# A fused attention and expert kernel on one core: first weights in quarters from SyncE, two sequences' pieces moved up, and a pair's scatters side by side

## The chip, the cores and the metric

The kernel runs on one core of a Trainium2 chip. The metric is the device time of one execution in microseconds. Three runs of the kernel before are the base: 709.80, 710.92 and 712.75 us, median 710.92. One more execution was taken with the hardware profiler; its trace gives every duration below.

The engines are called PE (TensorE), DVE (VectorE), ACT (ScalarE), POOL (GpSimd) and SP (SyncE, which issues most of the DMAs). Each runs its own instructions in order and waits on semaphores for the others.

## What is computed

Four sequences of 512 tokens with 256 features go through a conditional gated layer, attention with 16 heads that share one key and value head, a mixed linear layer, and a routed layer of eight experts. Cut to what matters:

```python
expert = argmax(cond_8)                       # one expert per sequence
hidden = silu(x @ Wu[expert].T + bu) * (x @ Wg[expert].T + bg)
c = hidden @ Wd[expert].T + bd                # 256 -> 512 -> 256
q, k, v = c @ Wq.T + bq, ...                  # 16 query heads, one k, one v
x = x + softmax(q k^T / 4) v @ Wo.T + bo
y = x @ mix(weight * mask, cond_8) + bias     # a weight matrix per sequence
probs = softmax(y @ w_router)                 # 8 experts, 2 per token
# in each of 8 groups of 256 tokens an expert takes at most 128 (token, choice) rows
out = x + sum over the kept choices of prob * (gelu(y @ wi[e]) @ wo[e])
```

The host lays out weights (transposes, halves side by side) before the launch; the arithmetic is on the chip.

## The kernel before, in words

All matrices are 32-bit floats. One mm() shows in the trace as two matmul passes and two weight loads.

**Start (lines 88 to 270).** SP loads the eight conditions of each sequence into cond_sb. DVE works out rows, the row numbers of each sequence's expert in the weight table (lines 109 to 117). fetch_cond(b) (line 137) lets POOL gather that expert's up and gate weights (1 MB, tile w, from the pool wi_sb) and its down weights with biases (0.5 MB, tile w2, shown as wo_sb) by an indirect DMA. For b = 0, 1 and 2 these come first on POOL, ahead of POOL's memsets and tables; b = 3 comes later, once tiles of b = 0 are free (wexp has three buffers). SP loads the four sequences of xT, the mask and the eight matrices w2_sb of the mixed layer, the small constants, and last writes zeros over the DRAM table xp (8,580 KB).

hidden(b, hc) makes a quarter of the hidden layer of a sequence: four mm into bank "a" (a single PSUM bank, line 262) and bank "x" (four banks, line 264), a SiLU on ACT (line 266), and a product on DVE (line 267). down(b, dc) (line 248) is the second matrix. Between them DVE mixes weights: mixed(b, g) (lines 235 and 237) adds one of eight masked matrices, which POOL has multiplied with the mask (line 227), into wb_sb. project(b) makes q, k and v of a sequence; SP copies the q rows into their place (line 314).

**Attention (64 steps).** A step n is a quarter of a unit u = n // 4 (four heads of a sequence). Each step runs maxima (PE line 354, DVE line 358) six steps ahead, exponentials (PE line 386, ACT line 387), and weigh of the step before (PE line 401, into bank "a"). At a unit's end its sums are copied to a tile called stage (line 409) and stored to od. shifted(u) (lines 368 and 372) turns the maxima of a unit and adds them to q; exponentials of that unit need its result qs.

Beside the steps run pieces of the neighbouring sequences. The list beside says which piece goes to which of a sequence's 16 steps, last the same for the last sequence (steps 48 to 63), where the pieces (-1, ...) are those of sequence 2. A sequence's chain is values, inv, norm, out, rT, mix (the mixed layer), choose and rank (the router, lines 529 to 567), places (a count by matmul, line 578), rows, send (POOL scatters the tokens to xp by expert, line 630, eight indirect DMAs). pairs is list_of_pairs: DVE lists the tiles of 256 rows (lines 797 to 850) that are full after three sequences, and SP reads the table into a register (lines 877 and 889) to fetch weights (line 870) and rows xt (line 892).

**Experts.** run() goes over units: six pairs (256 rows) of the first three sequences, then 14 single tiles (128 rows), then five more pairs. A unit is turn (PE line 925, DVE line 927), up (PE line 940, ACT line 944), and put for each half (PE line 970): DVE weighs the result (line 978), and POOL adds it to out_rows in DRAM by an indirect DMA (line 979). adds holds these DMAs: each waits for the one before, since both may touch the same rows. share(u) (lines 959 to 963) works out weights and the rows at. The last sequence's pieces go between the first pairs: place() is called twice in a unit's up and once after each put, and final says which pieces come at which call. Its piece rest makes the lists of the remaining tiles and lets the late fetches go.

Of the kernel before, what the change touches and what calls it, by code (L numbers as in the profile page):

```python
# [10 lines left out]
F32 = mybir.dt.float32  # L11
I32 = mybir.dt.int32
AF = mybir.ActivationFunctionType
# [4 lines left out]
P = 128  # L18
B = 4
T = 512  # L20
NT = B * T
D = 256
NE = 8
# [3 lines left out]
F = 1024  # L27
# [10 lines left out]
WROW = 1024 + 10  # L38
# [3 lines left out]
def adaln_attn_ffn_kernel(  # L42
# [34 lines left out]
    def bank(tag):  # L77
        return ps.tile([P, 512], F32, tag=tag, name=f"ps_{tag}", bufs=BANKS[tag])
# [11 lines left out]
    )  # L90


    rev = const.tile([P, NE], F32, name="rev")
    nc.gpsimd.iota(
        rev, pattern=[[-1, NE]], base=NE, channel_multiplier=0,
# [10 lines left out]
    rows = const.tile([P, B], I32, name="rows")  # L106
# [25 lines left out]
    def fetch_cond(b):  # L132

        w = wexp.tile([P, 2, F], F32, name="wi_sb").rearrange("p c f -> p (c f)")
        w2 = wexp.tile([P, F // P, D], F32, name="wo2_sb").rearrange("p c f -> p (c f)")
        for t, src in ((w, wcond), (w2[:, 0:WROW], wcond2)):
            nc.gpsimd.indirect_dma_start(
                out=t,
                out_offset=None,
                in_=src,  # L140
                in_offset=bass.IndirectOffsetOnAxis(ap=rows[:, b : b + 1], axis=0),
            )
        w_of.append((w, w2))

    for b in range(B):
        nc.sync.dma_start(xT_sb[:, :, ts(b, T)], xT[:, :, ts(b, T)])
        if b < 3:
            fetch_cond(b)
    nc.sync.dma_start(m2_sb, mask2.rearrange("p c o -> p (c o)"))
    for g in range(NE):  # L150
        nc.sync.dma_start(w2_sb[:, g, :], w2[:, g].rearrange("p c o -> p (c o)"))

    def load(ap, shape, name):
        t = const.tile(shape, F32, name=name)
        nc.sync.dma_start(t, ap)
        return t
# [95 lines left out]

    def hidden(b, hc):
        w, w2 = w_of[b]
        wu = w[:, 0:1024].rearrange("p (c h) -> p c h", c=2)
        wg = w[:, 1024:2048].rearrange("p (c h) -> p c h", c=2)
        if hc == 0:
            hid_of[b] = cp.tile([P, 4, T], F32, name="hid")
        pu = bank("a")
        pg = bank("x")  # L260
        for c in range(2):
            mm(pu, wu[:, c, ts(hc, P)], xT_sb[:, c, ts(b, T)], start=c == 0, stop=c == 1)  # L262
        for c in range(2):
            mm(pg, wg[:, c, ts(hc, P)], xT_sb[:, c, ts(b, T)], start=c == 0, stop=c == 1)  # L264
        sg = cp.tile([P, T], F32, name="sg", bufs=3)
        nc.scalar.activation(sg, pu, AF.Silu, bias=w2[:, 1024 + hc : 1025 + hc])
        nc.vector.scalar_tensor_tensor(  # L267
            hid_of[b][:, hc, :], pg, w2[:, 1028 + hc : 1029 + hc], sg, ALU.add, ALU.mult
        )

    for b in range(B - 1):
        for hc in range(4):
            hidden(b, hc)
            if (b, hc) > (1, 0):
                for _ in range(4):
                    mixed(*mixing.pop(0))
            if hc == 0 and b > 0:
                down(b - 1, 0)
                down(b - 1, 1)
# [9 lines left out]
    pa_of = {}  # L289
# [102 lines left out]
    def weigh(n, js):  # L392

        u, sc = divmod(n, 4)
        b, hg = divmod(u, 4)
        if u not in pa_of:
            pa_of[u] = bank("a")
        e = e_of[n]
        j0, nj = js[0], len(js)
        for hh in range(4):  # L400
            i = mm(  # L401
                pa_of[u][32 * hh : 32 * hh + 32, j0 * P : (j0 + nj) * P], seqs[b]["v"][:, sc, :],
                e[:, hh, j0 : j0 + nj].rearrange("p j n -> p (j n)"),
                start=sc == 0 and j0 > 0, stop=sc == 3 and j0 == 0,
            )
# [260 lines left out]
    def route_mixed(b):  # L666
# [58 lines left out]
    ON_PE = ("q", "k", "v", "out", "rT", "mix")  # L725
# [15 lines left out]
    def side(b, k):  # L741
# [38 lines left out]
    fp = attn_ctx.enter_context(tc.tile_pool(name="fp", bufs=2))  # L780
# [6 lines left out]
    pairs = fp.tile([P, 3, NE + 1], F32, name="pairs", bufs=1)  # L787
# [75 lines left out]
    reg, adds = {}, []  # L863
# [87 lines left out]
    def share(u):  # L951

        w = width(u)
        number, e0, p0, p1 = (xt_of[u][:, 0:w, D + k] for k in range(4))
        te = texp[:, u : u + 1]
        w0 = fp.tile([P, 2], F32, name="w0", bufs=3)[:, 0:w]
        w1 = fp.tile([P, 2], F32, name="w1")[:, 0:w]
        at = fp.tile([P, 2], I32, name="at", bufs=6)[:, 0:w]
        nc.vector.scalar_tensor_tensor(w0, e0, te, p0, ALU.is_equal, ALU.mult)
        nc.vector.scalar_tensor_tensor(w1, e0, te, p1, ALU.not_equal, ALU.mult)  # L960
        nc.vector.tensor_tensor(w0, w0, w1, ALU.add)  # L961
        nc.vector.tensor_scalar(w1, number, 0.0, spare1, ALU.is_equal, ALU.mult)  # L962
        nc.vector.scalar_tensor_tensor(at, number, -1.0, w1, ALU.add, ALU.add)  # L963
        shares[u] = w0, at

    def put(u, h):

        po = bank("x")
        for fc in range(F // P):
            mm(  # L970
                po[:, 0:D], hT_of[u][:, fc, ts(h, P)], wo_of[u][:, fc, :],
                start=fc == 0, stop=fc == F // P - 1,
            )
        if h == 0:
            share(u)
        w0, at = shares[u]
        y = fp.tile([P, D], F32, name="y", bufs=6)
        nc.vector.tensor_scalar(y, po[:, 0:D], w0[:, h : h + 1], None, ALU.mult)  # L978
        i = nc.gpsimd.indirect_dma_start(  # L979
            out=out_rows,  # L980
            out_offset=bass.IndirectOffsetOnAxis(ap=at[:, h : h + 1], axis=0),
            in_=y,
            in_offset=None,
            compute_op=ALU.add,
        )

        if adds:
            tc.add_manual_dep(i.ins, adds[-1].ins.name, AFTER, reason="same rows")
        if u < NA:
            tc.declare_no_dep(i.ins, group="last rows", reason="other sequences")  # L990
            tc.add_to_no_dep_group("early adds", i.ins)
        elif u == first_of_rest[0] and h == 0:
            for k in last_rows:
                tc.add_manual_dep(i.ins, k.ins.name, AFTER, reason="rows of the last sequence")
        adds.append(i)

    for n in range(STEPS + 1):
        m = n + LEAD
# [2 lines left out]
        b, k = divmod(n, 16)  # L1001
# [40 lines left out]
    places = itertools.count()  # L1042
# [71 lines left out]
def _layouts(i):  # L1114
# [32 lines left out]
    return {  # L1147
        "xT": halves(i["x"].reshape(NT, D).T),
        "cond": i["cond_8"].reshape(1, B * NE),
        "wcond": np.concatenate([up, gate], axis=1),  # L1150
        "wcond2": np.concatenate([down, b_up, b_gate, b_down], axis=1),
        "wq": halves(i["L0_attn_Wq"].T),
        "bq": i["L0_attn_bq"].reshape(2, P).T,
# [38 lines left out]
```

## Time and profile before

| what | us |
|---|---|
| median of three runs | 710.92 |
| the profiled execution | 722.33 |
| its span, first to last instruction | 720.50 |
| TensorE matmuls busy in the span | 669.3 |
| first matmul | 15.20 |
| first projection (line 307) | 72.48 |
| first unit of the experts (line 925) | 428.02 |
| end of the last matmuls | 703.2 |
| start of the last scatter (line 979) | 707.64 |

The profiled execution is 11.4 us longer than the median; it is set against its own parts. A row of the timeline gives the start and the time in us, the engine, the line, the operation with output<-input, its shape and count, and in brackets the engine's idle time before it with what ended that. In the 40 slices each stands for 18.0 us; a digit is the busy share in tenths, PEclk the granted TensorE clock.

### The profile page before, as it was taken

How to read it: one execution, taken by the hardware profiler on the slowest of the kernel's cores; microseconds unless marked ns; L12 is line 12 of the kernel's file. 1: busy time of each engine (PE TensorE's matmuls, PEld its weight loads, DVE VectorE, ACT ScalarE, POOL GpSimd, SP SyncE). 2: the span in 40 equal slices, each digit the busy share in tenths (PEclk: the TensorE clock that was granted, in tenths of full speed). 3: DMA queues.
4: the chain of work that ended last, by engine and by line, in shares of the span. 5: the costliest groups of instructions: out<-in, count | busy, mean ns of one | idle time of the engine just before them, and what ended most of it. 6: DMA issues, size and time to landing. Idle time of an engine off the chain costs nothing. (4 is left out here: it accounts for less than half of the span.)

```text
span 720.5 us, 10657 instructions
## 1 busy us (share of the span) xinstructions
PE 669.3 (93%) x4092; PEld 409.9 (57%) x4092; DVE 325.8 (45%) x760; ACT 226.8 (31%) x401; POOL 116.0 (16%) x119
## 2 busy tenths in 40 slices
PE   1999999999999999999989869999899999999990
PEld 0444433444344433453325338888799999988880
DVE  0246465566667693767766821536122222211210
ACT  0222113566554454455443642131111111121110
POOL 6600000000000013000400220126221112122221
PEclk9999899999999998999989989999999999999995
DMA  8997101100031104110221289734889999985321
GB/s 301 330 291 219 30 1 31 28 16 26 15 90 53 45 19 129 63 60 16 66 86 60 63 272 313 217 89 118 278 225 307 327 322 336 327 243 150 82 23 16
DMA packets 62184, 102.38 MB, mean 142 GB/s; under 512 B 6320, under 2 KB 26416, under 8 KB 61616
## 3 DMA queue, kind: packets, MB, share of 16 engines
q1 hardware_dynamic: 53840, 85.56, 36.7%
q0 software_dynamic: 7872, 15.29, 9.0%
q10 hardware_dynamic: 416, 0.79, 0.4%
q8 instruction: 34, 0.56, 0.3%
q14 instruction: 22, 0.18, 0.1%
HBM read 75.37 MB, written 24.15 MB: 138 GB/s over the span
## 5 line engine op out<-in xcount | busy, mean ns | idle before, releaser
L358 DVE TENSOR_REDUCE negm<-ps_m 128x1 f32<-128x512 f32 x250 | 160.9, 685 | 91.2 <-PE ps_x L386 69.2
L387 ACT ACTIVATE e<-ps_x 128x512 f32<-128x512 f32 x244 | 132.7, 595 | 130.7 <-PE ps_x L386 115.8
L354 PE MATMUL ps_m<-k,q 32*128 32x512 f32 x500 | 157.5, 651 | 5.4 <-DVE negm L358 3.4
L386 PE MATMUL ps_x<-qs,k 32*128 32x512 f32 x488 | 144.0, 657 | 0.3 <-DVE qs L372 0.3
L940 PE MATMUL ps_m<-xT,wi_sb 128*128 128x128 f32 (+1 forms) x800 | 132.0, 323 | 1.6 <-ACT e L944 0.8
L970 PE MATMUL ps_x<-wo_sb,e 128*128 128x256 f32 x576 | 130.0, 382 | 0.0
L940 PEld LDWEIGHTS ps_m<-xT,wi_sb 128*128 128x128 f32 x800 | 120.1, 193 | 12.2 <-ACT e L944 1.0
L970 PEld LDWEIGHTS ps_x<-wo_sb,e 128*128 128x128 f32 x576 | 108.6, 192 | 14.0
L944 ACT ACTIVATE e<-ps_m 128x512 f32<-128x512 f32 x72 | 42.9, 597 | 209.5 <-PE ps_m L940 203.4
L979 POOL DMA_INDIRECT out_dram<-y,at x36 | 55.8, 1550 | 211.2 <-DMA out_dram<-y,at 97.5
L354 PEld LDWEIGHTS ps_m<-k,q 32*128 32x128 f32 x500 | 45.9, 186 | 64.1 <-issue 29.3
L401 PE MATMUL ps_a<-e,v 128*32 128x256 f32 x1024 | 74.8, 392 | 2.7 <-ACT stage L409 2.3
L927 DVE COPY xT<-ps_a 128x256 f32<-128x256 f32 (+1 forms) x25 | 13.6, 542 | 117.7 <-PE ps_a L925 115.7
L401 PEld LDWEIGHTS ps_a<-e,v 128*32 128x32 f32 x1024 | 24.3, 109 | 73.4 <-issue 56.2
L978 DVE TENSOR_SCALAR y<-ps_x,w 128x256 f32<-128x256 f32 x36 | 17.4, 483 | 82.1 <-PE ps_x L970 80.9
L262 PE MATMUL ps_a<-xT_sb,wi_sb 128*128 128x512 f32 x64 | 34.1, 659 | 15.2 <-DMA wi_sb<-in_wcond_dram,rows 15.2
L386 PEld LDWEIGHTS ps_x<-qs,k 32*128 32x128 f32 x488 | 39.6, 188 | 5.2 <-issue 4.0
L562 POOL TENSOR_SCALAR x<-mk 128x4 f32<-128x4 f32 x4 | 0.8, 196 | 250.9 <-DVE mk L559 250.9
L630 POOL DMA_INDIRECT xp<-x,to_i x32 | 32.9, 1027 | 36.7 <-DVE to_i L627 20.5
L267 DVE SCALAR_TENSOR_TENSOR hid<-ps_x,wo_sb,sg 128x512 f32<-128x512 f32 x16 | 12.0, 750 | 54.7 <-PE ps_x L264 54.6
L262 PEld LDWEIGHTS ps_a<-xT_sb,wi_sb 128*128 128x128 f32 x64 | 12.8, 207 | 32.7 <-issue 17.5
L264 PE MATMUL ps_x<-xT_sb,wi_sb 128*128 128x512 f32 x64 | 31.0, 608 | 0.0
(149 smaller groups left out, 462.1 us busy)
## 6 DMA issues: line engine op xcount, KB each, us to landing
wi_sb<-in_wi_dram SPq DMA_DIRECT2D x25, 1024.0 KB
wo_sb<-in_wo_dram SPq DMA_DIRECT2D x25, 1024.0 KB
xp<-zeros SPq DMA_DIRECT2D x1, 8580.0 KB
od<-stage SPq DMA_DIRECT2D x15, 256.0 KB
xt<-xp SPq DMA_DIRECT2D x11, 260.0 KB
xT_sb<-in_xT_dram SPq DMA_DIRECT2D x4, 512.0 KB
w_sb<-in_w_dram SPq DMA_DIRECT2D x8, 256.0 KB
q<-stage SPq DMA_DIRECT2D x64, 32.0 KB
```

The source lines that it names most:

```text
L262: mm(pu, wu[:, c, ts(hc, P)], xT_sb[:, c, ts(b, T)], start=c == 0, stop=c == 1)
L264: mm(pg, wg[:, c, ts(hc, P)], xT_sb[:, c, ts(b, T)], start=c == 0, stop=c == 1)
L354: mm(pm, q[32 * j : 32 * j + 32, i, ts(hg, P)], k[32 * j : 32 * j + 32, :], start=True, stop=True,)
L358: nc.vector.tensor_reduce(nm[:, i, j, HD : HD + 1], pm, AX.X, ALU.max, negate=True)
L386: mm(px, k[rows_j, ts(sc, P)], qs_of[u][rows_j, :], start=True, stop=True)
L387: nc.scalar.activation(e_of[n][:, :, j, :].rearrange("p h (i t) -> p i h t", i=4), px.rearrange("p (i h t) -> p i h t", i=4, h=4), AF.Exp,)
L401: i = mm(pa_of[u][32 * hh : 32 * hh + 32, j0 * P : (j0 + nj) * P], seqs[b]["v"][:, sc, :], e[:, hh, j0 : j0 + nj].rearrange("p j n -> p (j ...
L630: i = nc.gpsimd.indirect_dma_start(out=xp, out_offset=bass.IndirectOffsetOnAxis(ap=to_i[:, k, ch : ch + 1], axis=0), in_=s["x3"][:, ch, 0: ...
L940: mm(ph[:, ts(k, n)], wi_of[u][:, c, ts(f0 + k, P)], xT_of[u][:, c, :], start=c == 0, stop=c == 1,)
L944: nc.scalar.activation(hT_of[u][:, f0 : f0 + each].rearrange("p f t -> p (f t)"), ph, AF.Gelu_apprx_tanh,)
L970: mm(po[:, 0:D], hT_of[u][:, fc, ts(h, P)], wo_of[u][:, fc, :], start=fc == 0, stop=fc == F // P - 1,)
L979: i = nc.gpsimd.indirect_dma_start(out=out_rows, out_offset=bass.IndirectOffsetOnAxis(ap=at[:, h : h + 1], axis=0), in_=y, in_offset=None, ...
```

## The change

Five edits. First, six matmuls of a zero tile and one SiLU are put at the head of the program. Second, the first sequence's weights no longer come by POOL's gather: SP reads the row number into a register and loads them in four quarters, each with all that one hidden(0, hc) needs, with the down weights after the first quarter; the host lays the table out in that order, for all sequences. SP's loads of x 1 move behind these, those of x 2 and 3 behind the matrices w2; the gathers of sequences 1 and 2 move behind POOL's memsets. Third, in last and final pieces move up by one or two places, and the last two units' stage is copied by DVE. Fourth, a pair's two scatters no longer wait for each other, only for both of the pair before. For that, fifth, the row numbers are made as floats and POOL copies each half into an integer tile of its own.

```diff
+    nil = const.tile([P, 512], F32, name="nil")
+    nc.vector.memset(nil, 0.0)
+    for _ in range(6):
+        mm(bank("x"), nil[:, 0:P], nil, start=True, stop=True)
+    nc.scalar.activation(const.tile([P, 1], F32, name="nil1"), nil[:, 0:1], AF.Silu)
...
-    for b in range(B):
+    def load_x(b):
         nc.sync.dma_start(xT_sb[:, :, ts(b, T)], xT[:, :, ts(b, T)])
-        if b < 3:
-            fetch_cond(b)
+    load_x(0)
+    row0 = nc.sync.value_load(rows[0:1, 0:1], min_val=0, max_val=(NE - 1) * P)
+    w, wd = cond_tiles()
+    for hc in range(4):
+        nc.sync.dma_start(w[:, ts(hc, 512)], wcond[ds(row0, P), ts(hc, 512)])
+        if hc == 0:
+            nc.sync.dma_start(wd[:, 0:WROW], wcond2[ds(row0, P), :])
+    load_x(1)
     nc.sync.dma_start(m2_sb, mask2.rearrange("p c o -> p (c o)"))
     for g in range(NE):
         nc.sync.dma_start(w2_sb[:, g, :], w2[:, g].rearrange("p c o -> p (c o)"))
+    load_x(2)
+    load_x(3)
...
+    fetch_cond(1)
+    fetch_cond(2)
     for g in range(NE):
         nc.gpsimd.tensor_tensor(w2_sb[:, g, :], w2_sb[:, g, :], m2_sb, ALU.mult)
...
-            mm(pu, wu[:, c, ts(hc, P)], xT_sb[:, c, ts(b, T)], start=c == 0, stop=c == 1)
+            mm(pu, wu[:, c, :], xT_sb[:, c, ts(b, T)], start=c == 0, stop=c == 1)
...
-            nc.scalar.copy(o, pa_of[u])
+            (nc.vector.tensor_copy if u >= 4 * B - 2 else nc.scalar.copy)(o, pa_of[u])
...
-        [(-1, "choose"), (-1, "rank0")],
-        [(-1, "rank1")],
+        [(-1, "choose"), (-1, "rank0"), (-1, "rank1")],
         [(-1, "places"), (-1, "rows"), (-1, "send")],
-        [(0, "values0"), (0, "pairs")],
+        [(0, "pairs")],
+        [(0, "values0")],
+        [(0, "bias")],
+        [(0, "pairs0")],
         [],
-        [(0, "pairs0")],
-        [(0, "bias")],
         [(0, "pairs1")],
...
-        0: ["inv0"], 2: ["values1"], 4: ["inv1", "norm0", "norm1"], 6: ["out0", "out1"],
-        7: ["out2", "out3"], 8: ["rT0", "rT1"], 9: ["mix0", "mix1", "mix2", "mix3"],
-        10: ["choose", "rank0"], 11: ["rank1"], 12: ["places", "rows", "send"], 13: ["rest"],
+        0: ["inv0"], 2: ["values1"], 4: ["inv1", "norm0", "norm1"],
+        6: ["out0", "out1", "out2", "out3"], 7: ["rT0", "rT1"],
+        8: ["mix0", "mix1", "mix2", "mix3"], 9: ["choose", "rank0"], 10: ["rank1"],
+        11: ["places", "rows", "send"], 12: ["rest"],
...
-        at = fp.tile([P, 2], I32, name="at", bufs=6)[:, 0:w]
+        at = fp.tile([P, 2], F32, name="at", bufs=3)[:, 0:w]
...
+        to = fp.tile([P, 1], I32, name="to_row", bufs=6)
+        nc.gpsimd.tensor_copy(to, at[:, h : h + 1])
...
-            out_offset=bass.IndirectOffsetOnAxis(ap=at[:, h : h + 1], axis=0),
+            out_offset=bass.IndirectOffsetOnAxis(ap=to, axis=0),
...
-        if adds:
-            tc.add_manual_dep(i.ins, adds[-1].ins.name, AFTER, reason="same rows")
+        for k in adds[-1] if adds else ():
+            tc.add_manual_dep(i.ins, k.ins.name, AFTER, reason="same rows")
+        if h > 0:
+            tc.declare_no_dep(i.ins, group=f"unit{u}", reason="other tokens")
+        tc.add_to_no_dep_group(f"unit{u}", i.ins)
...
-        adds.append(i)
+        now.append(i)
+        if h == width(u) - 1:
+            adds.append(list(now))
+            now.clear()
```

More of the change, by code (lines that the diff above doesn't have):

```diff
@@ L130, in adaln_attn_ffn_kernel, with cond_tiles, fetch_cond @@
     w_of = []
-    def fetch_cond(b):
+    def cond_tiles():
         w = wexp.tile([P, 2, F], F32, name="wi_sb").rearrange("p c f -> p (c f)")
         w2 = wexp.tile([P, F // P, D], F32, name="wo2_sb").rearrange("p c f -> p (c f)")
+        w_of.append((w, w2))
+        return w, w2
+    def fetch_cond(b):
+        w, w2 = cond_tiles()
         for t, src in ((w, wcond), (w2[:, 0:WROW], wcond2)):
@@ L142, in fetch_cond @@
             )
-        w_of.append((w, w2))
-    for b in range(B):
+    def load_x(b):
         nc.sync.dma_start(xT_sb[:, :, ts(b, T)], xT[:, :, ts(b, T)])
-        if b < 3:
-            fetch_cond(b)
+    load_x(0)
[6 more added lines that the diff above has]
+    load_x(1)
     nc.sync.dma_start(m2_sb, mask2.rearrange("p c o -> p (c o)"))
@@ L254, in hidden @@
         w, w2 = w_of[b]
-        wu = w[:, 0:1024].rearrange("p (c h) -> p c h", c=2)
-        wg = w[:, 1024:2048].rearrange("p (c h) -> p c h", c=2)
+        wu, wg = (
+            w[:, ds(512 * hc + 256 * n, 256)].rearrange("p (c h) -> p c h", c=2)
+            for n in range(2)
+        )
         if hc == 0:
@@ L261, in hidden @@
         for c in range(2):
-            mm(pu, wu[:, c, ts(hc, P)], xT_sb[:, c, ts(b, T)], start=c == 0, stop=c == 1)
+            mm(pu, wu[:, c, :], xT_sb[:, c, ts(b, T)], start=c == 0, stop=c == 1)
         for c in range(2):
-            mm(pg, wg[:, c, ts(hc, P)], xT_sb[:, c, ts(b, T)], start=c == 0, stop=c == 1)
+            mm(pg, wg[:, c, :], xT_sb[:, c, ts(b, T)], start=c == 0, stop=c == 1)
         sg = cp.tile([P, T], F32, name="sg", bufs=3)
@@ L862, in adaln_attn_ffn_kernel @@
     wi_of, wo_of, xt_of, xT_of, hT_of = {}, {}, {}, {}, {}
-    reg, adds = {}, []
+    reg, adds, now = {}, [], []
     AFTER = mybir.DependencyInfo(mybir.DependencyClass.Sync, mybir.DependencyReason.DATA)
@@ L1149, in _layouts @@
         "cond": i["cond_8"].reshape(1, B * NE),
-        "wcond": np.concatenate([up, gate], axis=1),
+        "wcond": np.stack([up, gate], axis=1)
+        .reshape(NE * P, 2, 2, 4, P)
+        .transpose(0, 3, 1, 2, 4)
+        .reshape(NE * P, 2048),
         "wcond2": np.concatenate([down, b_up, b_gate, b_down], axis=1),
```

## The prediction

> **What bounds the kernel now.** I read the page first (busy shares, slices, chain), then the timeline of TensorE at the places where it is not busy.
>
> ```profile
> span 720.5 us, 10657 instructions
> PE 669.3 (93%) x4092; PEld 409.9 (57%) x4092; DVE 325.8 (45%) x760; ACT 226.8 (31%) x401; POOL 116.0 (16%) x119
> PE   1999999999999999999989869999899999999990
> PEclk9999899999999998999989989999999999999995
> DMA  8997101100031104110221289734889999985321
> ```
>
> TensorE is busy 93% of the span, so a gain must come from the first slice, from the dips of slices 21 to 23 and 28, or from the last slice. The timeline names what ends each wait:
>
> ```profile
> 5.50 1.16 POOL L137 DMA_INDIRECT wi_sb<-in_wcond_dram,rows  x1 [4.35 <-DVE rows L117]
> 15.20 3.78 PE L262 MATMUL ps_a<-xT_sb,wi_sb 128*128 128x512 f32 x4 [15.20 <-DMA wi_sb<-in_wcond_dram,rows]
> ...
> 20.98 1.88 PE L262 MATMUL ps_a<-xT_sb,wi_sb 128*128 128x512 f32 x4
> ...
> 408.86 0.68 DVE L372 TENSOR_TENSOR qs<-ps_x,q 128x512 f32<-128x512 f32 x1
> 409.45 0.18 DVE L797 SCALAR_TENSOR_TENSOR cmp<-free,begin 128x32 f32<-128x32 f32 x1
> ...
> 428.02 0.63 PE L925 MATMUL ps_a<-ident,xt 128*128 128x128 f32 x4 [2.13 <-DMA xt<-xp]
> ...
> 514.90 0.69 PE L925 MATMUL ps_a<-ident,xt 128*128 128x128 f32 x2 [2.91 <-DMA xt<-xp]
> 515.38 8.42 PE L970 MATMUL ps_x<-wo_sb,e 128*128 128x256 f32 x32
> ...
> 702.71 1.55 POOL L979 DMA_INDIRECT out_dram<-y,at  x1 [2.98 <-DMA out_dram<-y,at]
> 703.21 0.48 DVE L978 TENSOR_SCALAR y<-ps_x,w 128x256 f32<-128x256 f32 x1 [2.97 <-PE ps_x L970]
> 707.64 1.54 POOL L979 DMA_INDIRECT out_dram<-y,at  x1 [3.38 <-DMA out_dram<-y,at]
> ```
>
> The reader is to see four places: 15.2 us without a matmul at the start, then four passes in 3.78 us where later ones take 1.88; 2.1 us at 428; 2.9 us at 515 followed by slow passes (8.42 us, where the same 32 take 7.07 at 498); and a last scatter that starts 3.9 us after its data are ready (703.69 to 707.64).
>
> [...]the starts of the first weight loads lie 0.85 us apart, from 20.1 us on 0.43. [...]its packets, sorted by queue and size, show the gather (8,192 B packets) moving about 320 KB per us and SyncE's loads (2,048 B) about 80, from 11 to 18 us. [...]here small ones take 2.0 us (od written at 399.82, read from 401.84) to 3.1 (cond issued 0.82, read 3.93).
>
> **Part 1, the start.** Before, the first weights are 1 MB by a GpSimd gather issued at 5.50; its packets begin at 10.2 and the first matmul starts at 15.20. At half rate hidden(0, ·) takes 15.20 to 30.85 = 15.65 us; at full rate it is 4 x 3.43 = 13.73, so 1.92 us are lost.
>
> After: rows are ready at 5.20 as now. From a table's write to the fetch that reads it, SyncE needs 1.17 us (L825 ends 411.40, fetch 412.57), so quarter 0 is issued at 6.4. A hardware-queue load shows its first packets 1.6 us after issue (xT: issue 1.28, packets 2.9); 256 KB at 300 to 330 KB/us are 0.8 us[...]. The nearest whole row, the xt load of 260 KB, takes 3.0 us from issue (425.02 to 428.02), which gives 9.4. I take 9.5, bounds 9.2 and 10.8.
>
> The zero matmuls are 6 x 2 passes. From about 1.4 us (a memset comes before) five or six run at 0.85 and the rest at 0.43, to about 8.4[...]. So the real ones start warm; cost beyond 9.5: 0 to 0.4 us. If zeros did not warm the array, 1.9 us come back.
>
> Then each piece takes 3.43 us. wd (0.5 MB) follows quarter 0 and lands near 11.3, when the first SiLU can start (bank "a", single, is wanted at 12.9). Quarter 1 lands at 12.1, wanted 12.9; quarters 2 and 3 at 12.9 and 14.5, wanted 16.4 and 19.8. The SiLU table is loaded ahead (1.28 us), which lay beside the matmuls already. The gathers of b = 1 and 2 now follow GpSimd's memsets (12.90 to 19.62 before, so 1.15 to 7.9), issue at 7.9, and move packets from 12.6; they leave SyncE a fifth of the rate (a third beside the 4,136 B ones), and x1 lands at 19.4, wanted 23.3. w1 lands near 17, wanted 23.3. mask, weights w2, x2, x3 follow: w2 ends near 29 instead of 26; the first four GpSimd products (1.24 us each) end by 30, VectorE wants them at 37.6. So hidden by the matmuls of sequence 0 and 1. If the cover is gone, VectorE's mixed() stands in front of hid and TensorE waits one for one.
>
> What is late next: the DMA engines stand idle from 4.6 to 8.0, so all that follows is about 3 to 4 us later; the zeros into xp (8.58 MB) ended at 67.3 and will end near 71. The q rows leave SyncE 7.6 us earlier, at 70.0 (77.61 before), on the same queue, and are caught behind the zeros for about 0.8 us. Part 1: 15.20 + 1.92 - 9.5 - 0.8 = 6.8 us gained, bounds 3.5 and 8.
>
> **Part 2, end of attention.** For the last sequence rank1 goes ahead of the last four maxima, places/rows/send one step up, list_of_pairs one step up and so ahead of shifted(15). VectorE works in order, and its sum is the same: choose starts 398.66, rank0 ends 401.1, rank1 takes 1.5, the four reductions 2.6, rows to send 3.3; only an idle 0.8 us before L591 goes. to_i is ready at 408.5 instead of 408.94, the eight scatters (1.28 us each, 5.6 from issue to landing) end 0.4 us earlier, and xt with them. Against it: maxima 63 wait 1.5 us for rank1, and qs (408.86 before) now stands behind the list (3.5 us): about 412.6, so that exponentials(60) wait 3.0 us. TensorE's end of attention had 2.1 us to spare before xt, and the copy of stage on VectorE (0.69) frees ScalarE of 0.6. Sum: -0.5 us, bounds -3 (qs delay not absorbed) and +4 (the wait of 2.1 and a half-rate window, 1.7, both gone). bias, pairs0 and values0 keep slack of many us (inv0 runs at 429); on SyncE, fetch_in(0) ahead of values0 delays those two loads from 402 to about 413.
>
> **Part 3, end of the last sequence beside the experts.** Each piece moves one place up, 3.5 us of matmuls. choose now follows y of unit 1 at about 476 and its exponential stands before the gelus of unit 3, not behind two (481.54): rank0 comes 4.9 us earlier, but places waits for its place in TensorE's order, 483.5 instead of 486.77. Send and the lists come 3.3 to 3.6 us earlier. The scatters land at 504.0 (507.3); the first late wi fetch goes at 496.3 (499.95). The wait at 514.90 is bandwidth: wi, wo, wi, wo, 4.2 MB, lie ahead of xt on the queue, 12.7 us at 330 KB/us. 3.6 us earlier they end near 511, xt lands at about 512, TensorE is there at 511.9. Gone: the 2.9 us and the half rate after it (8.42 - 7.07 and 0.69 - 0.38, 1.65 us): 4.3 us, bounds 1.5 (wo(6) waits for put(3), 504.9, so not all loads move) and 4.6.
>
> **Part 4, the tail.** The two scatters of a pair wait for the pair before, not for each other. Now: 693.62, 698.18, 702.71, 707.64, some 4.7 apart. Then: 693.6, 697.1, 701.5, and 704.1 after y at 703.69. GpSimd's 36 copies of the index (0.2 us, as its small copies at L567) lie in its idle time. 3.5 us less, 0.2 for the copy: 3.3, bounds 2.3 (two adding at once land more slowly) and 3.6. No other put is on TensorE's path: y has six buffers.
>
> **Sum.** 6.8 - 0.5 + 4.3 + 3.3 = 13.9 us. The profiled execution took 722.33 us (span 720.5, 1.8 around it), 11.4 more than the median 710.92; I take the same gain off both: 708.4 profiled, 697.0 as the median.
>
> **Rivals.** (a) All parts, as above: 697. Chance 0.55. (b) The start gives half: quarter 0 lands at 10.8, quarter 1 behind it is late, or the q rows wait for the zeros. For it: the packets of 2 to 9 us run at only 300 KB/us and the zeros end so near. Start 3.5 instead of 6.8, so 700.3. Chance 0.2. (c) The end of attention gains as well, with its half-rate window gone: +4 instead of -0.5: 692.5. For it: the clock was at half from about 416 to 419 and 429 to 433. Against: VectorE's order. Chance 0.15. (d) No difference: the start and parts 2 and 3 are given back to new waits (start 3.5, part 2 -3, part 3 +1.5, tail 2.3 = 4.3, less one more half-rate window of 3.4): 710. Chance 0.06. (e) Slower: the w2 weights, behind the register wait and two gathers on SyncE's queue, hold GpSimd's products, these VectorE's mixed(), and that hid and TensorE at L262. It costs nothing until product 3 is later than 37.6 (I expect 30); to undo all it must be 8 + 14 us late, about 52, and a further 4 us gives 715. For it: packets of 2 KB get a fifth beside a gather. Against: only 3.1 MB of gathers, done by 24. Chance 0.04.
>
> **How the numbers follow.** Predicted is (a), 697. The range 690.5 to 703.5 takes in (b), (c) and one half-rate window (3.4 us, as at 81 to 88) either way. The runs before spread by 0.4%, so 0.5% (3.6 us) is about what can be told: faster 0.90 (a, b, c), same 0.06 (d), slower 0.04 (e).
>
> **What would show it.** Right: first L262 near 9.5 us with passes of 0.43 at once; first projection (L307) near 65; no wait at L925 on the first single unit and no slow L970 after it; last scatter within 1 us of its y. Wrong: L262 waits again at quarter 1 or at L248; L354 waits for q long after 72; qs (L372) behind the list with a TensorE wait over 3 us; xt of the first single still waiting 2 us or more.

## The result and the profile after

The changed kernel takes 703.65 us (median of four runs, 703.59 to 704.92), the kernel before 711.47 (four runs, 709.80 to 712.75). The ratio is 0.9896, with a 95% interval from 0.9871 to 0.9920: 7.8 us are gained where 13.9 were forecast, and the time lies 0.15 us above the upper end of the forecast range, 703.5.

The profile of the kernel after, its page and slices (17.5 us each):

```profile
span 701.9 us, 10770 instructions
PE 666.7 (95%) x4104; PEld 410.0 (58%) x4104; DVE 329.9 (47%) x763; ACT 225.8 (32%) x400; POOL 120.8 (17%) x153
PE   6999999999999999999999969999899999999992
PEclk8999999999999999999999979999999999999996
DMA  5999201100022103220131388634889999984322
```

The first slice of TensorE is now at 6 instead of 1, but 7.0 us of that are zeros. The dips of slices 21 to 23 have become one, that of slice 28 is left, and the last slice has some work in it. Line numbers have moved: the hidden layer is at 287 and 289, the first projection at 332, maxima at 379, turn at 952, up at 967, put at 997, the scatter-add at 1008. The timeline of the same kernel at the places that the prediction named:

```profile
1.54 7.02 PE L96 MATMUL ps_x<-nil 128*128 128x512 f32 x12 [1.54 <-DVE nil L94]
4.26 3.56 POOL L243 MEMSET q<- 128x2048 f32 x2
4.66 0.19 DVE L123 TENSOR_REDUCE top<-first 128x4 f32<-128x32 f32 x1
4.95 2.89 DVE L124 TENSOR_SCALAR rows<-top,rowp 128x4 int32<-128x4 f32 x1
8.14 1.14 POOL L149 DMA_INDIRECT wi_sb<-in_wcond_dram,rows  x1 [0.32 <-DVE rows L124]
8.89 0.37 SPq L164 DMA_DIRECT2D wi_sb<-in_wcond_dram  x1
14.03 3.75 PE L287 MATMUL ps_a<-xT_sb,wi_sb 128*128 128x512 f32 x4 [5.46 <-DMA wi_sb<-in_wcond_dram]
21.21 1.95 PE L287 MATMUL ps_a<-xT_sb,wi_sb 128*128 128x512 f32 x4 [1.31 <-DMA wi_sb<-in_wcond_dram]
...
72.78 3.60 PE L332 MATMUL ps_x<-coT,wq_sb 128*128 128x512 f32 x8
...
414.17 1.09 PE L952 MATMUL ps_a<-ident,xt 128*128 128x128 f32 x4 [4.64 <-DMA xt<-xp]
...
501.38 0.44 PE L952 MATMUL ps_a<-ident,xt 128*128 128x128 f32 x2 [1.87 <-DMA xt<-xp]
501.66 7.07 PE L997 MATMUL ps_x<-wo_sb,e 128*128 128x256 f32 x32
...
688.15 0.48 DVE L1007 TENSOR_SCALAR y<-ps_x,w 128x256 f32<-128x256 f32 x1 [2.97 <-PE ps_x L997]
688.15 0.76 POOL L1005 CAST to_row<-at 128x1 int32<-128x1 f32 x1
689.40 1.55 POOL L1008 DMA_INDIRECT out_dram<-y,to_row  x1 [0.48 <-POOL to_row L1005]
```

The first real matmul starts at 14.03 us, not at 9.5, takes 3.75 us for four passes, at half rate again (1.95 for the four at 21.21), and quarter 1 is waited for as well (1.31). The first projection comes at 72.78: before it came at 72.48, so the start gained nothing. The row that explains it is the fourth: the row numbers take 2.89 us. In the profile of the kernel before the same operation takes 0.23, with the memset of q far behind it:

```profile
4.97 0.23 DVE L117 TENSOR_SCALAR rows<-top,rowp 128x4 int32<-128x4 f32 x1
...
16.09 3.55 POOL L222 MEMSET q<- 128x2048 f32 x2
```

At 501 a wait of 1.87 is left, but the slow passes after it are gone (7.07). The last scatter starts 0.77 us after its y is ready (688.63), where it was 3.95 before.

The profiled execution of before that the prediction is drawn from took 722.33 us, 10.9 more than the median of its runs. A second profile of that kernel (below, b1_before) has a span of 709.9 us and fits the median; the parts are compared with that one.

### The profile page after: what moved, and what is told of

Same layout as the page of the kernel before. It is cut to its first block, busy times and chain, and to the rows that moved or that the text cites. A ratio compares the mean times of both kernels' runs of the same rounds, so it can differ in the third digit from the quotient of the medians.

```text
span 701.9 us, 10770 instructions
## 1 busy us (share of the span) xinstructions
PE 666.7 (95%) x4104; PEld 410.0 (58%) x4104; DVE 329.9 (47%) x763; ACT 225.8 (32%) x400; POOL 120.8 (17%) x153
## 4 chain that ended last, share of the span: by engine, by line
PE 85%; DMA 5%; DVE 5%; issue 2%; POOL 1%; SPq 0%; ACT 0%; POOLq 0%; DVEq 0%
PE ps_m L379 18%; PE ps_m L967 17%; PE ps_x L997 17%; PE ps_a L426 8%; PE ps_a L287 4%; PE ps_x L271 4%; PE ps_x L289 4%; PE ps_x L538 2%; PE ps_x L332 2%; PE ps_x L506 2%; DMA wi_sb<-in_wcond_dram 2%; DVE negm L383 2%; PE ps_x L411 1%; DMA xt<-xp 1%; PE ps_x L393 1%
## 5 line engine op out<-in xcount | busy, mean ns | idle before, releaser
L379 PE MATMUL ps_m<-k,q 32*128 32x512 f32 x500 | 151.1, 639 | 1.9 <-DVE negm L383 1.6
L411 PE MATMUL ps_x<-qs,k 32*128 32x512 f32 x488 | 140.3, 643 | 0.1
L997 PE MATMUL ps_x<-wo_sb,e 128*128 128x256 f32 x576 | 128.5, 379 | 0.0
L1008 POOL DMA_INDIRECT out_dram<-y,to_row x36 | 56.0, 1555 | 129.1 <-DVE at L990 34.0
L656 POOL DMA_INDIRECT xp<-x,to_i x32 | 32.6, 1018 | 44.6 <-DVE to_i L653 20.5
L1005 POOL CAST to_row<-at 128x1 int32<-128x1 f32 x36 | 20.1, 557 | 74.3 <-DVE at L990 74.3
```

The costliest lines, as they stand in the source:

```text
L379: mm(pm, q[32 * j : 32 * j + 32, i, ts(hg, P)], k[32 * j : 32 * j + 32, :], start=True, stop=True,)
L411: mm(px, k[rows_j, ts(sc, P)], qs_of[u][rows_j, :], start=True, stop=True)
L656: i = nc.gpsimd.indirect_dma_start(out=xp, out_offset=bass.IndirectOffsetOnAxis(ap=to_i[:, k, ch : ch + 1], axis=0), in_=s["x3"][:, ch, 0: ...
L997: mm(po[:, 0:D], hT_of[u][:, fc, ts(h, P)], wo_of[u][:, fc, :], start=fc == 0, stop=fc == F // P - 1,)
L1008: i = nc.gpsimd.indirect_dma_start(out=out_rows, out_offset=bass.IndirectOffsetOnAxis(ap=to, axis=0), in_=y, in_offset=None, compute_op=AL ...
```

## The experiments

Three groups were run, each beside the kernel before on one chip; the chip of the first group is another than that of the other two. In the first group that kernel took 721.76 us, in the second 711.08, in the third 712.44. Only ratios are compared across groups, medians within one.

### The parts alone, put into the kernel before

**b0_before** is the kernel before, unedited.

> The kernel before, unchanged, for a second profile: the first one took 722.3 us, 11 more than its median. Theory A (the first profile held chance stalls of attention): the span is near 710, the first projection again starts near 72.5, and the two half-rate windows of 6.8 us at 279 and 361 us are shorter or gone, so that the first unit of the experts starts near 416 to 420 instead of 428. Rival: the profile costs 11 us by itself; then the span is near 720 again.

It took 720.77 us. Its span is 719.1, near the first profile's 720.5; the first projection comes at 73.29. So the span near 710 did not come back here, but the profile doesn't cost 11 us by itself either: all runs of this kernel in this group have a median of 721.76.

**p1_start** has the first two edits only (zeros and SiLU, quarters with their layout, gathers behind the memsets); attention, experts and tail are as before.

```diff
+    for _ in range(6):
+        mm(bank("x"), nil[:, 0:P], nil, start=True, stop=True)
...
+    row0 = nc.sync.value_load(rows[0:1, 0:1], min_val=0, max_val=(NE - 1) * P)
+    for hc in range(4):
+        nc.sync.dma_start(w[:, ts(hc, 512)], wcond[ds(row0, P), ts(hc, 512)])
...
+    fetch_cond(1)
+    fetch_cond(2)
```

> The start alone (zero matmuls, quarters from SyncE, gathers behind the memsets). Theory A: it gains nothing, ratio 0.998 to 1.003 (0 to -1 us), since VectorE's rows instruction waits 2.7 us for GpSimd's memset of q and the gathers then starve the quarters; first projection near 72.8. Rival: it gains 4 to 5 us (ratio 0.993 to 0.995) and the moves gain little; the first projection near 68.

721.17 us, ratio 1.0015 (0.9990 to 1.0039). No gain of the start alone is seen, at most 0.7 us by the interval. Its trace has the same rows as the changed kernel: the row numbers take 2.89 us from 4.96, quarter 0 is issued at 8.90, the first matmul starts at 13.59, and the first projection at 72.77. So the loss before the first projection needs no later part.

Behind that the trace shows something else. By projection 3 p1_start is 4.3 us ahead of b0_before (264.14 and 268.44), 3.4 of it because a stretch at half rate near 81 us, 6.8 us long in b0_before, is missing; why it is missing isn't shown. At the first single unit the lead is taken back in part: xt is waited for 4.43 us instead of 2.83, and the 32 passes behind it take 9.79 us instead of 8.68. TensorE reaches this place 2.6 us earlier, xt comes only 1.0 us earlier (511.69 and 512.73).

**p23_moves** has the third edit only (last, final, the copy of stage).

```diff
+            (nc.vector.tensor_copy if u >= 4 * B - 2 else nc.scalar.copy)(o, pa_of[u])
...
+        [(-1, "choose"), (-1, "rank0"), (-1, "rank1")],
...
+        11: ["places", "rows", "send"], 12: ["rest"],
```

> The moved pieces alone (the lists last and final, stage copied by VectorE). Theory A: most of what the tail does not explain, 3 to 5 us, ratio 0.993 to 0.996, from the wait at the first single unit, which is gone or under 2 us, without a half-rate window after it. Rival: nothing, 0.999 to 1.002, because the scatters to xp still end last before the first unit.

719.43 us, ratio 0.9977 (0.9959 to 0.9995): 1.7 us gained, 0.4 to 3.0 by the interval, where the sum of these two parts was 3.8 and 3 to 5 were expected here. The wait at the first single unit is down to 0.48 us, with passes at full rate behind it (7.07). But several engines stop near 421 us (VectorE idles 7.12), at the end of attention, and the first unit starts at 431.82, where it is 425.87 in b0_before. Such stops come up again in the last section.

**p4_tail** has the fourth edit and the index copies that it needs.

```diff
+        to = fp.tile([P, 1], I32, name="to_row", bufs=6)
+        nc.gpsimd.tensor_copy(to, at[:, h : h + 1])
...
+        for k in adds[-1] if adds else ():
+            tc.add_manual_dep(i.ins, k.ins.name, AFTER, reason="same rows")
```

> Two scatters of a pair at once, alone. Theory A: 3.3 us, ratio 0.9954 (0.994 to 0.997), the last scatter starting 1.3 us after the last matmul instead of 4.5, and nothing else changed. Rival: two adds at once land later and GpSimd's copies delay others, gain under 1.5 us.

717.83 us, ratio 0.9944 (0.9924 to 0.9963): 4.0 us, 2.7 to 5.5 by the interval. The three parts alone add up to 4.6 us, less than the 7.8 of the whole, though the intervals don't set the two apart. The trace of this part shows its gain directly: TensorE ends at 705.27 and the last scatter starts at 706.56, 1.29 us later; in the first profile of before these are 703.18 and 707.64, 4.46 apart.

### What holds the row numbers

**c_after** is the changed kernel again, unedited, so that the next three can be set beside it.

> The changed kernel, unchanged, beside the three below. Theory A (pauses of all engines while POOL scatters tokens to xp are the chip's and not the change's: they are in every profile of 720 us and in none of 702): if this chip runs the kernel before in 717 to 727 us, this profile shows three or four pauses of 3 to 5 us in the scatter bursts too, and its time is near 714; the ratio stays 0.989 to 0.993. Rival: the change removes the pauses; then none here, and the time is near 704 on any chip.

705.04 us, ratio 0.9909 (0.9888 to 0.9930), span 702.0. The kernel before takes 711.08 us in this group, so the condition of the first theory isn't met; there are no pauses in the trace, and the run doesn't tell the two apart.

**a_stt** computes the same row numbers, with one operation of VectorE in another form. The column rowp is given as a broadcast tensor, not as the second scalar.

```diff
-    nc.vector.tensor_scalar(rows, top, -float(P), rowp, ALU.mult, ALU.add)
+    nc.vector.scalar_tensor_tensor(
+        rows, top, -float(P), rowp.to_broadcast([P, B]), ALU.mult, ALU.add
+    )
```

> The changed kernel with one instruction in another form: rows by scalar_tensor_tensor (two inputs in SBUF) instead of tensor_scalar. Theory A (the tensor_scalar [...]waits for the memset of q): rows takes 0.2 us instead of 2.89, the first quarter is issued at 6.3 to 6.5 instead of 8.89, the first real matmul starts at 9.3 to 10.5, warm, and the first projection near 66 to 68 instead of 72.8; 4 to 6 us less than c_after. Rival (rows waits for a semaphore or for the row numbers rowp): no change, first matmul at 14.0.

696.99 us (695.42 to 697.66), ratio 0.9788 (0.9764 to 0.9812): 8.05 us less than c_after, more than the 4 to 6 expected. The timeline of a_stt:

```profile
4.26 3.56 POOL L245 MEMSET q<- 128x2048 f32 x2
...
5.01 0.16 DVE L124 SCALAR_TENSOR_TENSOR rows<-top,rowp 128x4 int32<-128x4 f32 x1
...
6.22 0.37 SPq L166 DMA_DIRECT2D wi_sb<-in_wcond_dram  x1
...
7.99 1.14 POOL L151 DMA_INDIRECT wi_sb<-in_wcond_dram,rows  x1 [0.18 <-issue]
...
10.14 1.96 PE L289 MATMUL ps_a<-xT_sb,wi_sb 128*128 128x512 f32 x4 [1.46 <-DMA wi_sb<-in_wcond_dram]
11.93 1.88 PE L291 MATMUL ps_x<-xT_sb,wi_sb 128*128 128x512 f32 x4
...
65.15 3.60 PE L334 MATMUL ps_x<-coT,wq_sb 128*128 128x512 f32 x8
```

The memset of q has not moved, but the row numbers take 0.16 us beside it. In the changed kernel the same operation ends at 7.84, and the memset at 7.82. The reduction at 4.66 takes 0.19 us beside the memset. So beside it the tensor_scalar is held to its end, and neither a tensor_reduce nor the scalar_tensor_tensor is; what the two engines contend for is not shown. The row holds two memsets of 1.81 us each, back to back, and the tensor_scalar, which came during the first, waited for both. In the kernel before, the memset runs from 16.09, since six gathers stand ahead of it, and the tensor_scalar takes 0.23 us. So it is the change's own move of the gathers that brought the two together. Semaphores and the row numbers rowp are as they were in a_stt, so the rival, a wait for one of them, falls.

What the 2.7 us cost beyond themselves can be read from the DMA view. The two queues (packets, MB, share of the 16 engines' time), first 13 to 16 us of the kernel after, then 10 to 13 us of a_stt, in each case the time after quarter 0:

```profile
DMA packets 242, 1.18 MB, mean 392 GB/s; under 512 B 18, under 2 KB 18, under 8 KB 180
q0 software_dynamic: 142, 0.78, 64.1%
q1 hardware_dynamic: 100, 0.40, 33.0%
```

```profile
DMA packets 480, 1.05 MB, mean 350 GB/s; under 512 B 54, under 2 KB 54, under 8 KB 468
q1 hardware_dynamic: 468, 0.95, 94.1%
q0 software_dynamic: 12, 0.10, 8.4%
```

In the kernel after, the gather of sequence 1 is issued at 8.14, ahead of quarter 0 at 8.89, and its packets (q0) take two thirds of the engines' time while quarters 1 to 3 and the down weights are due: hence, in all likelihood, the wait of 1.31 us at 21.21, which a_stt hasn't. In the first profile of before SyncE's loads moved 0.18 of 0.84 MB beside a gather in packets of 8,192 B (11 to 13 us) and 0.12 of 0.40 beside one in packets of 4,136 B (19.5 to 20.5): the fifth and, nearly, the third of the prediction. In a_stt quarter 0 leads by 1.8 us, and SyncE's loads (q1) have the engines nearly to themselves: with 0.59 MB from 7 to 10 us they reach 1.54 MB by 13, about the 1.5 MB of all quarters and the down weights. The third loss is the clock. Stretches of the two kernels (busy times of PE, PEld, DVE, ACT, POOL, then the granted clock, the DMA share and GB/s); the kernel after:

```profile
8.00:11.00 3.00, 0.56 (x2) 0.00 (x0) 0.00 (x0) 0.00 (x0) 2.25 (x3) 1.00 0.31 74
11.00:14.00 3.00, 0.00 (x0) 0.01 (x1) 0.00 (x0) 0.00 (x0) 1.72 (x2) 0.61 0.91 329
14.00:18.00 4.00, 3.97 (x5) 1.84 (x6) 0.00 (x0) 0.00 (x0) 0.00 (x0) 0.50 1.00 405
```

and a_stt:

```profile
8.00:11.00 3.00, 1.54 (x4) 0.49 (x3) 0.00 (x0) 0.00 (x0) 2.39 (x3) 1.00 0.80 261
11.00:14.00 3.00, 3.00 (x8) 1.33 (x7) 0.08 (x1) 0.69 (x1) 1.57 (x2) 1.00 1.04 375
```

In the kernel after the zeros end at 8.56, with 5.5 us of nothing behind them: the granted clock falls from 1.00 to 0.50 at 11.6 and stays there until 18.5. In a_stt the gap is 1.46 us and the clock stays at 1.00. In the kernel after the zeros warm nothing (the first real passes run at 0.50), because the loads that they were to cover come too late.

**a_stt_nozero** is a_stt without the zero tile, its six matmuls and the early SiLU.

```diff
-    for _ in range(6):
-        mm(bank("x"), nil[:, 0:P], nil, start=True, stop=True)
-    nc.scalar.activation(const.tile([P, 1], F32, name="nil1"), nil[:, 0:1], AF.Silu)
```

> As a_stt without the six zero matmuls, their memset and the SiLU ahead. Theory A: the real matmuls start at the same time and at half rate for 3.4 to 6.8 us, so 1.7 to 3 us are lost against a_stt, and the SiLU table costs up to 1.3 more where the first bank is waited for. Rival: the zeros do not help, since TensorE falls back to half rate before the weights come; no difference.

699.52 us, ratio 0.9833 (0.9805 to 0.9861). With the quarters in time the zeros and the early SiLU are worth 2.5 us together. First matmul at 9.94, at half rate (four passes in 3.75), first projection at 67.36, 2.2 later than in a_stt.

### The end of attention

**a_no2** is the changed kernel with last and the copy of stage as before.

```diff
-            (nc.vector.tensor_copy if u >= 4 * B - 2 else nc.scalar.copy)(o, pa_of[u])
+            nc.scalar.copy(o, pa_of[u])
...
-        [(-1, "choose"), (-1, "rank0"), (-1, "rank1")],
+        [(-1, "choose"), (-1, "rank0")],
+        [(-1, "rank1")],
```

> The changed kernel with the pieces of the attention's end as before (the list last, and stage copied by ScalarE). Theory A (part 2 brings under 1 us, since the scatters to xp start at the same time): within 0.2% of c_after. Rival: part 2 brings what the sum of the others lacks, 2 to 4 us, and this kernel is that much slower.

705.06 us, ratio 0.9898 (0.9876 to 0.9920); c_after took 705.04. No worth of part 2 is seen, and the intervals leave some 2 us either way. In both kernels TensorE waits for xt before the first unit (6.12 us from attention's last matmuls to 416.44 in a_no2, 4.64 in the kernel after). The profile of a_no2 is late before this stretch already (projection 3 at 268.73, 265.9 in c_after); from there to the first unit it takes 147.7 us, c_after 148.1.

### The last sequence's pieces

**b1_before** is the kernel before, unedited.

> The kernel before once more, for a profile of it beside kernels of the fast kind. Theory A: where the kernel before runs in 709 to 714 us, its profile has no pauses of all engines in the scatter bursts at 274, 358 and 411, its first projection is at 72.5 as in the first profile, and its first unit of the experts starts at 414 to 418. Rival: the pauses are there and the profile alone costs 10 us.

711.65 us, span 709.9. Its timeline, to be set against that of the kernel after:

```profile
72.37 3.60 PE L307 MATMUL ps_x<-coT,wq_sb 128*128 128x512 f32 x8
...
415.84 1.09 PE L925 MATMUL ps_a<-ident,xt 128*128 128x128 f32 x4 [6.76 <-DMA xt<-xp]
...
504.00 0.44 PE L925 MATMUL ps_a<-ident,xt 128*128 128x128 f32 x2 [2.94 <-DMA xt<-xp]
504.27 8.76 PE L970 MATMUL ps_x<-wo_sb,e 128*128 128x256 f32 x32
...
692.44 0.48 DVE L978 TENSOR_SCALAR y<-ps_x,w 128x256 f32<-128x256 f32 x1 [2.97 <-PE ps_x L970]
697.05 1.54 POOL L979 DMA_INDIRECT out_dram<-y,at  x1 [3.51 <-DMA out_dram<-y,at]
```

**a_no3** is the changed kernel with final as before.

```diff
-        6: ["out0", "out1", "out2", "out3"], 7: ["rT0", "rT1"],
-        8: ["mix0", "mix1", "mix2", "mix3"], 9: ["choose", "rank0"], 10: ["rank1"],
-        11: ["places", "rows", "send"], 12: ["rest"],
+        6: ["out0", "out1"],
+        7: ["out2", "out3"], 8: ["rT0", "rT1"], 9: ["mix0", "mix1", "mix2", "mix3"],
+        10: ["choose", "rank0"], 11: ["rank1"], 12: ["places", "rows", "send"], 13: ["rest"],
```

> The changed kernel with the last sequence's pieces beside the experts placed as before (the list final). Theory A: the wait at the first single unit is 2.9 us and more instead of 1.9 to 2.2, with half-rate passes after it; 1 to 3 us slower than c_after. Rival: part 3 brings nothing, since the loads ahead of the rows are bandwidth; within 0.5 us of c_after.

709.54 us, ratio 0.9965 (0.9951 to 0.9980). Against c_after's 0.9909 of another group that is 0.0056 of 711 us, 4.0 us, more than the 1 to 3 expected; the spans differ by 5.1 (707.1 and 702.0). The timeline of a_no3:

```profile
503.79 0.69 PE L951 MATMUL ps_a<-ident,xt 128*128 128x128 f32 x2 [4.42 <-DMA xt<-xp]
504.27 9.74 PE L996 MATMUL ps_x<-wo_sb,e 128*128 128x256 f32 x32
```

Without the move the wait is 4.42 us instead of 1.87, and the half rate after it costs 9.74 - 7.07 = 2.67: together 5.2, against 5.1 between the spans. Up to the first unit the two are alike (414.20 and 414.02). The move takes the clock's loss away and more than half of the wait. The wait of a_no3 is also longer than the 2.94 of b1_before: TensorE gets there 1.7 us earlier, and xt at nearly the same time (503.79 and 504.00). As in p1_start, what is gained earlier is lost here unless the rows come earlier too.

Why is 1.9 left? SyncE's queue in the kernel after:

```profile
484.04 0.38 SPq L897 DMA_DIRECT2D wi_sb<-in_wi_dram  x1
484.66 0.37 SPq L897 DMA_DIRECT2D wo_sb<-in_wo_dram  x1
486.43 0.38 SPq L897 DMA_DIRECT2D wi_sb<-in_wi_dram  x1
492.64 0.37 SPq L897 DMA_DIRECT2D wo_sb<-in_wo_dram  x1
494.11 1.54 SPq L919 DMA_DIRECT2D xt<-xp  x2
```

The last load of wo waits until 492.64 for its buffer, and both loads of xt stand behind it in the program. In a_no3 that load is issued at 492.50, so the move did not bring it forward: in both kernels it goes right after the put of unit 3 has ended (at 492.61 in the kernel after). The first wi and the first wo came 2.1 us earlier (486.10 and 486.72 there), the second wi 1.5 (487.92).

**a_rows_first** is a_stt with the rows of the first single unit fetched ahead of that load of wo.

```diff
-    def run(units, rows):
+    def run(units, rows, early=lambda k: ()):
...
+            for x in early(k):
+                fetch_rows(units[x])
             for x in units[k + 2 : k + 3]:
                 fetch(fetch_out, x)
...
-            return NA, NA + 1
+            return (NA + 1,)
...
-    run(units, rows_behind)
+    run(units, rows_behind, lambda k: (NA,) if k == NA - 2 else ())
```

> a_stt, and the rows of the first single unit are fetched ahead of the down weights of its own unit (1 MB less in front of them). Theory A (the wait at that unit is the 4.2 MB of weights in front on the queue): the wait of 1.7 us is gone, 1.5 to 2 us less than a_stt, about 695.3. Rival: the rows wait for the scatters into xp; no gain, or the weights come late at the unit's put.

694.97 us, ratio 0.9756 (0.9737 to 0.9774), 0.0032 or 2.3 us under a_stt, whose interval, of another group, touches this one; the trace is the better witness. On the queue xt is issued at 486.85 and wo at 487.65, and on TensorE the unit starts without a wait:

```profile
487.67 6.85 PE L969 MATMUL ps_m<-xT,wi_sb 128*128 128x256 f32 x31
494.36 0.38 PE L954 MATMUL ps_a<-ident,xt 128*128 128x128 f32 x2
```

**a_rows_wi1** does the same at the end of attention: the rows of the first two pairs are fetched ahead of the second wi.

```diff
-            i = fetch_in(1)
-            tc.add_manual_dep(i.ins, weighed[-1].ins.name, AFTER, reason="not at once")
             fetch_rows(0)
             fetch_rows(1)
+            i = fetch_in(1)
+            tc.add_manual_dep(i.ins, weighed[-1].ins.name, AFTER, reason="not at once")
```

> a_rows_first, and the rows of the first two pairs are fetched ahead of the second pair's up weights (1 MB). Theory A (the scatters' landing, 6.7 us after issue, is stretched by that load): the wait before the first unit falls from 4.4 us by 0.5 to 1.5 us. Rival: the landing is the scatters' own; no change, and the second unit waits for its weights.

692.04 us (690.80 to 694.34), ratio 0.9718 (0.9695 to 0.9742), 2.9 us under a_rows_first in the same group. The first unit's 32 passes over wi (line 969), which start at half rate in both, take 8.97 us instead of 10.22, and the second unit does not wait for its weights. The wait before the first unit goes from 4.67 us (a_rows_first) to 3.06:

```profile
406.64 1.09 PE L954 MATMUL ps_a<-ident,xt 128*128 128x128 f32 x4 [3.06 <-DMA xt<-xp]
```

This version beats both kernels, the changed one by 1.8 to 1.9% (0.9718 against 0.9896 and 0.9909).

## Why the prediction was wrong, step by step

Progress of four traces, from the first instruction (us):

| | first hidden | projection 0 | projection 3 | first unit | first single | last matmul ends | last scatter |
|---|---|---|---|---|---|---|---|
| b1_before | 14.87 | 72.37 | 267.4 | 415.84 | 504.00 | 692.41 | 697.05 |
| c_after | 14.06 | 72.81 | 265.9 | 414.02 | 501.4 | 688.13 | 689.42 |
| a_stt | 10.14 | 65.15 | 259.5 | 407.94 | 494.79 | 681.51 | 682.80 |
| a_rows_wi1 | 10.06 | 65.07 | 258.2 | 406.64 | 491.08 | 677.75 | 679.03 |

**Part 1 failed, at its first step.** "After: rows are ready at 5.20 as now", and from it "quarter 0 is issued at 6.4", "the real ones start warm", and "Quarter 1 lands at 12.1". I moved the memsets of GpSimd ahead of its gathers in the sum, and took VectorE's rows as untouched, since the two have no data in common. Beside the memset they took 2.89 us instead of 0.23, and a_stt (0.16 beside the same memset) shows that the form of the operation decides: rows at 7.84, quarter 0 at 8.89, behind a gather at 8.14, first matmul at 14.03 and at half rate, quarter 1 late (1.31). First projection 0.4 us later than in b1_before instead of 6.8 earlier. The bounds of 3.5 and 8 left this out. By projection 3 the kernel is 1.5 us ahead after all, since the half rate near 81 us lasts 3.4 us instead of 6.8. The forecast held nothing of this; that the new start is its cause isn't shown (in p1_start, with the same start, that half rate is missing altogether).

With that one instruction in its other form, the steps of part 1 hold: quarter 0 issued at 6.22 (6.4), first matmul at 10.14 (9.5, up to 0.4 more), passes at full rate at once, no wait for quarter 1, first projection at 65.15 (near 65), and the median of a_stt is 696.99 against the 697.0 forecast. So the failed step is large enough for the whole miss of 6.65 us (703.65 against 697.0): 8.05 us between the medians of c_after and a_stt in one group, 6.7 between their spans. That the sum is met so closely is luck: in a_stt part 3 brings less than forecast, and the start and the stretch up to projection 3 more. Price of the zeros: 1.9 us were said to come back without them, 2.5 are measured, with the early SiLU gone as well. The zeros were to end near 8.4; the passes and rates named there add up to some 8.7 to 9.1, and they ended at 8.56. The q rows behind the zeros of xp cost 0.37 us in a_stt (0.8 was said).

**Part 2 was right in sum**: -0.5 us forecast, 0.0 between the medians of a_no2 and c_after, whose intervals are some 1.5 us wide to either side. The parts of that sum did not come as forecast: counted from projection 3, to_i, the rows that the scatters into xp need, comes 1.1 us earlier in the kernel after than in a_no2 and the first unit doesn't; qs comes 2.4 us later, behind the list on VectorE (393.92 to 397.50), and the exponentials that need it were to wait 3.0 us, but they start at 398.15, right behind qs (398.10), without a wait. The 2.1 us to spare before xt were read in the first profile; in b1_before TensorE waits 6.76 there.

**Part 3 was right in size, not in its picture.** 4.3 us were forecast, 4.0 follow from the ratios of a_no3 and c_after (some 1.8 either way). That is luck in part: the wait was to shrink by 2.9 us and the half rate to give 1.65 back, and the traces show 2.55 and 2.9 (2.67 for the put, 0.25 for the turn), from a longer wait. Within the kernel before, together with part 2, it gave only 1.7 us (at most 3.0), so its worth depends on what is around it. Forecast was that xt lands as TensorE comes; in fact it waits 1.87 to 2.15 us there, because the rows stand behind the load of wo on SyncE. The prediction had the four loads ahead of xt, named the last as what might not move, and let the whole queue move by 3.6 us all the same; in fact the loads moved by 2.1, 2.1, 1.5 and 0 us. a_rows_first shows that the order on the queue is what holds the rows.

**Part 4 was right**: 3.3 us forecast, 4.64 - 1.29 = 3.35 by the traces of b1_before and c_after. The last scatter starts within 1 us of its y, as forecast (0.77). The copy of the index was priced at 0.2 us; right behind a scatter it takes 0.76 to 0.79, of which 0.3 is on the path.

**The sum by stages.** b1_before to c_after: start -0.4, from projection 0 to 3 +1.9, to the first unit +0.3, to the first single +0.8, to the last matmul +1.7, tail +3.3, in all 7.6 of the 7.9 us by which the spans differ. b1_before to a_stt in the same stages: 7.2, 0.7, 0, 1.3, 1.7, 3.35: 14.3.

The 1.7 to the last matmul are the slow passes behind the first single unit that are gone. Of the rivals, (b), half of the start lost, came nearest in time (700.3) with the right signs (the quarters late) and a cause that it did not name. For (e) there is nothing in the traces.

## What to carry to other kernels

When a piece of work moves on one engine's queue, list what then runs at the same moment on the other engines, not only what waits for its data: here a tensor_scalar of VectorE on the path, the row numbers, took 2.89 us beside a memset of GpSimd, and as scalar_tensor_tensor 0.16. A warm-up and an early load belong together: with 1.46 us between the zeros and the real matmuls the granted clock stayed at 1.00, with 5.5 us it was at 0.50 when they began. Time gained early is worth only what the next wait leaves of it: a_no3 reaches the first single unit 1.7 us before b1_before and waits 1.5 us longer there (4.42 and 2.94), since its rows come at nearly the same time (503.79 and 504.00); so the rows have to move as well. On SyncE's queue the small load that is wanted next goes ahead of the large one that waits for a buffer: placed behind such a wo (492.64), xt was issued at 494.11 and waited for 1.87 us; placed ahead of it, in a_rows_first, it was issued at 486.85 and not waited for.

## What the runs showed that was not expected

- A tensor_scalar on 4 elements per partition took 2.89 us beside a memset of GpSimd and 0.23 without; as scalar_tensor_tensor 0.16 beside the same memset. That the form of the instruction decides is what a_stt shows; by what mechanism, no run shows.
- In the kernel after the granted clock fell from 1.00 to 0.50 at 11.6 us, 3.1 us after the end of the last zero matmul (8.56), and was back at 1.00 at 18.5, 4.4 us after the first real one (14.03).
- In the traces with spans near 720 us (the first of before, b0_before and the three parts alone) several engines stop at once, VectorE for 4.4 to 4.7 us near 360, while GpSimd issues the eight scatters into xp or right after. The first profile of before, an example:

```profile
362.10 1.89 DVE L358 TENSOR_REDUCE negm<-ps_m 128x1 f32<-128x512 f32 x3 [4.68 <-remote]
362.18 1.08 ACT L387 ACTIVATE e<-ps_x 128x512 f32<-128x512 f32 x2 [3.53 <-remote]
```

"remote" means that the profile shows no releaser on the core. In b1_before, the kernel after and c_after there is no such stop. In the first profile of before the stops and the half rate after them come to some 10 us, an estimate from TensorE's idle time beside b1_before (3.7 us more) and from the clock (0.83 from 270 to 290 us and 0.89 from 340 to 370, so 6.7 us), and its parts in attention could not be set against the changed kernel's. What causes them was not settled: the first group's chip has them in all its profiles, the other in none.
- The wait for the q rows near 74 us is 0.37 us in a_stt, 2.22 in a_rows_first and 1.64 in a_rows_wi1, though the three are the same program up to there; why is not shown.
